# Spreading the second image's bottleneck samples over 210 samples of the next layer, with the image and offsets that follow moved after them

## The chip, the cores and the metric

The kernel runs on one core of one Trainium2 chip. The metric is the device time of one execution in microseconds (us). The core has five engines that this text names by their short names: PE (TensorE, matmuls), DVE (VectorE), ACT (ScalarE), POOL (GpSimd) and SP (SyncE, which only issues transfers here). Each runs its own instructions strictly in order and waits for the others by semaphores.

## The reference: what is computed

Four layers run one after another on two images (`B = 2`) of 256 channels and 64 x 64 pixels, in float32:

- L0: group norm, self-attention with 4 heads over the 4096 pixels, projection, residual.
- L1: a position term is added.
- L2: a bottleneck. A 1x1 convolution to 64 channels, then a 3x3 deformable convolution with a mask, a 1x1 convolution back to 256 channels, residual, ReLU.
- L3: two deformable convolutions of 256 channels, each behind a group norm and ReLU, and a residual at the end.

The part that this case is about is the deformable convolution. For each output pixel and each of 9 taps it samples the input at a learned place between pixels:

```python
out = gather(y0, x0) * (wy0 * wx0)[:, None] + gather(y0, x0 + 1.0) * (wy0 * wx1)[:, None] + gather(y0 + 1.0, x0) * (wy1 * wx0)[:, None] + gather(y0 + 1.0, x0 + 1.0) * (wy1 * wx1)[:, None]
```

The samples of all taps are then multiplied with the weights. The places come from an offset convolution over the normalised input.

## The kernel before, in words

The program has two stages. `attention` does L0 and L1 and, in its gaps, the bottleneck (L2) of image 0 and the first part of the bottleneck of image 1. `deform` does L3, and within it the rest of the bottleneck of image 1. The change is in `deform` alone.

**The samples.** `deform` is one loop over `s`. One value of `s`, called a sample here, is 128 pixels at one tap. A block of 512 pixels has 4 x 9 = 36 samples (`BLOCK = 36`), an image has 8 blocks, so one deformable convolution of one image has 288 samples (`LAYER = 288`). There are four of these: image 0 and image 1 of the first convolution, then both again for the second, 1152 samples in all. In iteration `s` the loop issues `gather(s + 8)` (four neighbours of 128 pixels, 512 KB, into one of 10 buffers `four`), `left(s + 3)` on ACT (line 1471), `right(s + 2)` on DVE (1477), `first(s + 1)` on ACT (1486), `others(s)` on DVE (1490 or 1496), two transposes of a sample on PE (1508), every fourth time a copy on ACT (1517), and the product with the weights on PE (1527). `left` and `right` exist for "paired" samples only; an unpaired one costs DVE three instructions of line 1496.

The first 72 samples (`EARLY * BLOCK`) were already gathered during the attention. They are loaded by plain transfers from `samp_d` (line 1448), and are unpaired. All later samples of the loop are gathered by POOL: one indirect transfer each (line 848).

**The side work.** Other work is written as generators and wrapped in `Side`. In each iteration `follow(s)` takes steps from the generator until their count reaches `rate * (s - start) + more(s)`. Nothing else schedules it: the order on each engine is the order in which the loop issues it.

- `second` is `Bottleneck.conv(1, ...)`, the deformable sampling of the bottleneck of image 1. It has 144 tiles of four neighbours. A tile is two indirect transfers on POOL into `bfour` (line 848), issued 7 tiles ahead, then three DVE instructions (1067, 1077, 1078), here called a weighing. It takes 7 steps for the first 7 tiles, then two steps per tile: one that issues the gather of the tile 7 further on and the first DVE instruction, one that issues the other two. Every 18 tiles, a block, products on PE and six more DVE instructions (1123, 1129, 1130) follow.
- `last` computes the places of the last two blocks of the same bottleneck, one step per sample.
- `offsets(b, l)` computes the places and shares of the next samples, 24 steps per block (`OFFS = 24`): 14 matmul steps (line 805), then seven small matmuls (825), four more (839) and small DVE arithmetic, ending in the indices `didx` (768). For image 0 of the first convolution it runs beside the samples at 24/36 of a step per sample. The next one in line, for image 1, begins at sample 228 at the same rate, so it ends at sample 516.
- `image(b, l)` loads and normalises an image (ACT, 1372), transposes it (PE, 1382), copies it (DVE, 1388) and writes it out to DRAM as `img3` (1394), from where the gathers read. For image 1 it begins when `second` is done, because it reuses its buffers (`inner.close()`) and needs its statistics.

Before the change `second` follows `0.9 s + 2.5 min(s, 72)`: 3.4 steps per sample over the first 72, then 0.9. It has about 300 steps, so its last tile is weighed at sample 127 and it ends at about sample 137. The image of image 1 follows at 0.9 of a step per sample, up to about sample 198.

Of the kernel before, what the change touches and what calls it, by code (L numbers as in the profile page):

```python
# [29 lines left out]
EARLY = 2  # L30
# [34 lines left out]
class Net:  # L65
# [1235 lines left out]
    def deform(self, bott):  # L1301
# [5 lines left out]
        with ExitStack() as ctx:  # L1307
# [19 lines left out]
            def load(b, src, pool):  # L1327
                x[b] = pool.tile([P, 2, HW], F32, name=f"x{b}")
                src = src.rearrange("(cb p) n -> p cb n", p=P)
                for i in range(4):  # L1330
                    cols = slice(1024 * i, 1024 * i + 1024)
                    queue = (nc.gpsimd, nc.sync)[b]
                    queue.dma_start(x[b][:, :, cols], src[:, :, cols])
# [3 lines left out]
            def offset_weights(l):  # L1337

                queue = (nc.gpsimd, nc.sync)[l]
                dw = wp.tile([P, 2, T], F32, name="dw")  # L1340
                queue.dma_start(dw, a["dw"][l])
                pw = wp.tile([P, 2, 2 * K2], F32, name="pw")
                queue.dma_start(pw, a["pw"][l])
                yield
                yield
                self.wf = wp.tile([P, 2, T, 2 * K2], F32, name="wf")
                for cb in range(2):
                    self.filters(self.wf[:, cb], cb, dw, pw)
                    yield
# [10 lines left out]
            def image(b, l):  # L1360

                if l == 0:
                    load(b, self.x2d[b], ctx.enter_context(tc.tile_pool(name="df_x1", bufs=1)))
                sc, sh = yield from self.norm_steps(
                    stats[b], bott.gmask, V_GN_G[l], V_GN_B[l], ps
                )
                yield
                v = self.img3[b].rearrange("(y x) (s c) -> y x s c", x=GW, c=C)
                for i in range(NB):
                    for cb in range(2):  # L1370
                        xs = x[b][:, cb, 512 * i : 512 * i + 512]
                        nc.scalar.activation(
                            xs, xs, AF.Relu, scale=sc[:, cb : cb + 1], bias=sh[:, cb : cb + 1]
                        )
                        yield
                    t = work.tile([P, 4, C], F32, name="imgt")
                    for g in range(2):
                        pt = ps([P, 2, C])
                        for j in range(2):
                            px = (4 * i + g * 2 + j) * P  # L1380
                            for cb in range(2):
                                nc.tensor.transpose(
                                    pt[:, j, cb * P : cb * P + P],
                                    x[b][:, cb, px : px + P],
                                    self.ident,
                                )
                        yield
                        nc.vector.tensor_copy(t[:, g * 2 : g * 2 + 2, :], pt)
                        if g == 1:
                            for r in range(2):  # L1390
                                for s in range(2):
                                    y0 = 8 * i + r + 1 - s
                                    dst = v[y0 : y0 + 7 : 2, 1 : W + 1, s, :]
                                    nc.sync.dma_start(
                                        dst.rearrange("j x c -> x j c"),
                                        t[64 * r : 64 * r + 64, :, :],
                                    )
                        yield

            IMAGE = 4 + 6 * NB + 1  # L1400
            corners = {(0, 0, i): (None, w4, None) for i, w4 in self.early.items()}

            def offsets(b, l):
                if b == 0:
                    yield from offset_weights(l)
                wf = self.wf
                for i in range(EARLY if (b, l) == (0, 0) else 0, NB):
                    idx = cp.tile([P, 4, K2], I32, name="didx")
                    w4 = cp.tile([P, 4, K2, 4], F32, name="dw4")
                    w = cp.tile([P, 2, 4, K2, 2], F32, name="dwt")  # L1410
                    corners[b, l, i] = idx, w4, w
                    yield from self.offsets(
                        i,
                        [x[b][:, cb, :] for cb in range(2)],
                        lambda s, row: wf[:, s, DWK * row : DWK * row + DWK, :].rearrange(
                            "p t o -> p (t o)"
                        ),
                        self.vec[:, V_PWB + l : V_PWB + l + 1],
                        base, idx, w4, work, ods[i % 2], pd, w=w,
                    )  # L1420
# [5 lines left out]
            layers = [(b, l) for l in range(2) for b in range(B)]  # L1426
            BLOCK = 4 * K2
            LAYER, ALL = NB * BLOCK, len(layers) * NB * BLOCK
            AHEAD, LEAD = 8, BLOCK + 16
# [8 lines left out]
            def gather(s):  # L1438
                if s < ALL:
                    n, i, k, j = parts(s)  # L1440
                    b, l = layers[n]
                    fours[s] = gp.tile([P, 4, C], F32, name="four")
                    four = fours[s].rearrange("p s c -> p (s c)")
                    if n == 0 and i < EARLY:

                        queue = nc.gpsimd if s < AHEAD else nc.sync
                        m = 4 * k + j
                        queue.dma_start(four, self.samp_d[i][m * P : m * P + P, :])
                        return
                    idx = corners[b, l, i][0]  # L1450
                    self.gather(four, self.img3[b], idx[:, j, k : k + 1])
# [15 lines left out]
            def left(s):  # L1467

                if paired(s):
                    uv = fours[s][:, 0:2].rearrange("p s c -> p (s c)")  # L1470
                    nc.scalar.mul(uv, uv, share(s, 0, 1))  # L1471

            def right(s):
                if paired(s):
                    four = fours[s].rearrange("p s c -> p (s c)")
                    uv = four[:, : 2 * C]
                    nc.vector.scalar_tensor_tensor(  # L1477
                        uv, four[:, 2 * C :], share(s, 1, 1), uv, ALU.mult, ALU.add
                    )
# [103 lines left out]
            OFFS = 24  # L1583
            inner = ExitStack()
            second = bott.conv(1, bott.pools(inner, 8, 7), ps)
# [7 lines left out]
            offs = [Side(EARLY * BLOCK - LEAD - 6, OFFS / BLOCK, begun)]  # L1593
# [1 line left out]


            last = Side(0, 1, bott.last(1, bott.kept, ps))
            seconds = Side(0, 0.9, second, lambda s: 2.5 * min(s, EARLY * BLOCK))
            stats[0] = self.norm_stats()
            images = []  # L1600
            for s in range(ALL + 12):
                n = s // LAYER
                if s == LAYER:
                    stats[1] = self.norm_stats()
                gather(s + AHEAD)
                left(s + 3)
                right(s + 2)
                first(s + 1)
                others(s)
                if (s - 6) % 4 == 0:  # L1610
                    evacuate((s - 6) // 4)
                product(*divmod(s - 7, 4), s)
                turn(s - 2)
                for f in due.pop(s, ()):
                    f()
                last.follow(s)
                if seconds:
                    seconds.follow(s)
                    if not seconds.steps:
                        seconds = None  # L1620
                        stats[1] = bott.stats[1]
                        inner.close()
                        images.append(Side(s, 0.9, image(*layers[1])))
                if s % LAYER == LAYER // 2 and 1 <= n < len(layers) - 1:
                    images.append(
                        Side(s, IMAGE / (LAYER // 2 - LEAD - 12), image(*layers[n + 1]))
                    )
                if s % LAYER == LAYER - LEAD - 8 and n + 1 < len(layers):
                    for o in images + offs:
                        for _ in o.steps or ():  # L1630
                            pass
                    images, offs = [], []
                    offs.append(Side(s, OFFS / BLOCK, offsets(*layers[n + 1])))
                for o in images + offs:
                    o.follow(s)

# [100 lines left out]
```

## Time and profile before

| what | value |
|---|---|
| median of three runs | 5140.26 us (5137.35 to 5144.84) |
| the profiled execution | 5136.46 us, span of the profile 5134.7 us |
| PE busy | 4802.3 us (94%) |
| DVE busy | 4012.2 us (78%) |
| ACT busy | 3255.6 us (63%) |
| POOL busy | 2336.0 us (45%) |

How to read it: line numbers are lines of the kernel before. Issuing a transfer counts as busy on POOL only where POOL itself builds it (lines 848, 1448, 1333, 1358). Line 1486 has one instruction per sample, 1152 in all, so the start of the n-th one, in order of time, says when sample n is reached. That gives this table, which the text uses to turn samples into times:

| sample | starts at, us from the start of the span |
|---|---|
| 0 | 2989.5 |
| 12 | 3036.8 |
| 72 | 3319.1 |
| 132 | 3492.6 |
| 204 | 3625.8 |
| 288 | 3759.7 |
| 432 | 3986.6 |
| 516 | 4126.0 |

### The profile page before, as it was taken

Reading aid. Unit: us, or ns where it says so; the run is one execution under the profiler, and the core shown is the slowest. Engines: PE = TensorE matmul, PEld = TensorE weight load, DVE = VectorE, ACT = ScalarE, POOL = GpSimd, SP = SyncE. Lnnn points to the kernel's source line nnn. Section 1 sums busy time; section 2 is a strip of 40 time slices with the busy share of each in tenths; the row PEclk is TensorE's granted clock in tenths of the full one; section 3 lists DMA queues with packets and bytes.
Section 4 is the critical chain, followed back from the end, with each engine's and each line's share of the span. In section 5 each row is a group of like instructions: output and inputs, shape, how many; then the busy total and the mean of one; then the engine's idle time right before and its main releaser. Section 6 shows DMA issues by size and latency. Waiting matters only on the chain. (4 is left out here: it accounts for less than half of the span.)

```text
span 5134.7 us, 100400 instructions
## 1 busy us (share of the span) xinstructions
PE 4802.3 (94%) x38200; PEld 2665.6 (52%) x38200; DVE 4012.2 (78%) x7281; ACT 3255.6 (63%) x5869; POOL 2336.0 (45%) x2256
## 2 busy tenths in 40 slices
PE   8999999999999999999999956679999999999998
PEld 5555565555565555565555523234444444454444
DVE  6878767878768888677766768867788888888888
ACT  5676656666667666666656622257876766666666
POOL 0111111111106777564023257775776666666665
PEclk9999999999999999999999978889999999999999
DMA  5231121111112333322557667679999999999998
GB/s 172 61 97 52 43 69 49 35 47 30 55 53 85 100 100 103 96 84 74 158 172 277 251 237 238 204 243 359 349 327 341 358 368 349 359 401 345 350 353 329
DMA packets 367026, 997.69 MB, mean 194 GB/s; under 512 B 61372, under 2 KB 98810, under 8 KB 366542
## 3 DMA queue, kind: packets, MB, share of 16 engines
q0 software_dynamic: 196560, 690.41, 37.7%
q1 hardware_dynamic: 169438, 300.73, 18.0%
q8 instruction: 300, 4.92, 0.4%
q14 instruction: 184, 1.51, 0.1%
q10 hardware_dynamic: 544, 0.13, 0.0%
HBM read 855.36 MB, written 127.35 MB: 191 GB/s over the span
## 5 line engine op out<-in xcount | busy, mean ns | idle before, releaser
L598 ACT ACTIVATE e<-sc,low 128x1024 f32<-128x1024 f32 x1024 | 1147.3, 1120 | 739.1 <-DVE low L592 736.2
L848 POOL DMA_INDIRECT four<-img,didx x1080 | 1163.2, 1077 | 558.1 <-issue 132.8
L592 DVE TENSOR_REDUCE low<-sc 128x1 f32<-128x1024 f32 x1024 | 1204.5, 1217 | 229.9 <-PE sc L580 225.3
L1527 PE MATMUL out<-st,wc 128*128 128x512 f32 x2304 | 1234.0, 618 | 118.2 <-ACT st L1517 100.7
L580 PE MATMUL sc<-k,qs 64*128 64x512 f32 x2048 | 998.0, 605 | 1.8 <-ACT e L598 1.4
L639 PE MATMUL av<-et,v 128*64 128x256 f32 x8192 | 996.6, 385 | 0.0
L580 PE MATMUL sc<-k,q 64*128 64x512 f32 x2048 | 977.0, 604 | 0.0
L519 POOL TENSOR_TENSOR o<-o,f 128x1024 f32<-128x1024 f32 x63 | 149.6, 2375 | 1763.4 <-DMA f<-share_d 966.5
L610 PEld LDWEIGHTS tt<-ident,e 64*128 64x128 f32 x16384 | 654.5, 139 | 512.4 <-issue 271.6
L629 ACT COPY et<-tt 128x512 f32<-128x512 f32 x1152 | 659.5, 585 | 171.4 <-PE tt L610 170.3
L1496 DVE SCALAR_TENSOR_TENSOR smp<-four,dw,smp 128x256 f32<-128x256 f32 x1296 | 627.2, 484 | 176.0 <-ACT smp L1486 144.9
L610 PE MATMUL tt<-ident,e 64*128 64x64 f32 x16384 | 726.5, 226 | 35.5 <-ACT et L629 18.3
L627 DVE COPY et<-tt 128x512 f32<-128x512 f32 x896 | 611.6, 683 | 161.7 <-PE tt L610 161.3
L639 PEld LDWEIGHTS av<-et,v 128*64 128x64 f32 x8192 | 553.2, 137 | 300.7 <-issue 47.8
L1508 PEld LDWEIGHTS pt<-ident,smp 128*128 128x128 f32 x2304 | 330.1, 144 | 661.6 <-issue 458.5
L848 POOL DMA_INDIRECT bfour<-img,bidx x576 | 583.5, 1013 | 183.5 <-issue 90.6
L1527 PEld LDWEIGHTS out<-st,wc 128*128 128x128 f32 x2304 | 389.9, 195 | 388.6 <-issue 201.2
L1471 ACT ACTIVATE four<-four,dwt 128x512 f32<-128x512 f32 x648 | 463.5, 715 | 192.6 <-DMA four<-img,didx 188.8
L1477 DVE SCALAR_TENSOR_TENSOR four<-four,dwt 128x512 f32<-128x512 f32 x648 | 483.8, 747 | 105.5 <-ACT four L1471 103.2
L1508 PE MATMUL pt<-ident,smp 128*128 128x128 f32 x2304 | 448.9, 277 | 27.2 <-DVE smp L1496 26.0
L580 PEld LDWEIGHTS sc<-k,qs 64*128 64x128 f32 x2048 | 346.2, 188 | 209.1 <-issue 116.3
L805 PE MATMUL pd<-x,wf 128*126 128x512 f32 x840 | 435.1, 600 | 0.0
(189 smaller groups left out, 4738.1 us busy)
## 6 DMA issues: line engine op xcount, KB each, us to landing
f<-share_d SPq DMA_DIRECT2D x128, 256.0 KB
four<-samp_d SPq DMA_DIRECT2D x64, 512.0 KB
xb<-xn SPq DMA_DIRECT2D x55, 512.0 KB
img<-imgt SPq DMA_DIRECT2D x96, 256.0 KB
four<-img,didx POOLq DMA_INDIRECT x1080
xa<-res SPq DMA_DIRECT2D x32, 512.0 KB
samp_d<-xb SPq DMA_DIRECT2D x32, 512.0 KB
xb<-in_x SPq DMA_DIRECT2D x20, 512.0 KB
```

The lines of the kernel that those rows point to most:

```text
L580: nc.tensor.matmul(s[:, j, :], lhsT=q[u, i // 2][int(h != j)][halves[j], at : at + P], rhs=k[u][c][halves[j], h, :], start=True, stop=True,)
L592: nc.vector.tensor_reduce(low, s, AX.X, ALU.max, negate=True)
L598: nc.scalar.activation(e.rearrange("p j n -> p (j n)"), s, AF.Exp, bias=blk.low[:, g, c : c + 1], accum_out=blk.sum[:, g, c : c + 1],)
L610: nc.tensor.transpose(pt[:, m, :], e[half, m // 4, m % 4 * P : m % 4 * P + P], self.ident[half, half],)
L627: nc.vector.tensor_copy(dst, pt)
L629: nc.scalar.copy(dst, pt)
L639: nc.tensor.matmul(now["av"][halves[h], :], lhsT=v[u][c][:, m, halves[h]], rhs=ets[j][:, m, h, :], start=(m == 0), stop=(m == 7),)
L848: self.nc.gpsimd.indirect_dma_start(out=dst, out_offset=None, in_=img, in_offset=bass.IndirectOffsetOnAxis(ap=idx, axis=0),)
L1477: nc.vector.scalar_tensor_tensor(uv, four[:, 2 * C :], share(s, 1, 1), uv, ALU.mult, ALU.add)
L1496: nc.vector.scalar_tensor_tensor(smps[s], four[:, c], weight(s, c), smps[s], ALU.mult, ALU.add)
L1508: nc.tensor.transpose(pts[u][:, c, j * P : (j + 1) * P], smp[:, c * P : c * P + P], self.ident,)
L1527: nc.tensor.matmul(outs[ob], lhsT=wc[k][:, c, ob * P : ob * P + P], rhs=sts[u][:, c, :], start=(k == 0 and c == 0), stop=(k == K2 - 1 and ...
```

## The change

Three paces are changed, all of side work in `deform`; no instruction's size or engine is.

- `second` follows a pace of its own: 8 steps at once at sample 0, none until sample 10, 1.95 per sample up to sample 72 (129 steps by then), then 1.25 per sample. By it the last tile's gather is issued at about sample 197, its last weighing at sample 206, and `second` ends at about sample 212.
- The image of image 1 follows at `IMAGE / (OPEN - END)` = 53/48 = 1.10 steps per sample, from about sample 212 to 261.
- The offsets of image 1 begin at sample 262 (`OPEN`) and no longer at 228: the 24 steps of the first block in 16 samples, the rest at 0.85 per sample, so they end at about sample 476. The later layers' offsets keep their start and rate.

```diff
-            seconds = Side(0, 0.9, second, lambda s: 2.5 * min(s, EARLY * BLOCK))
+            HELD, END, OPEN = 10, 214, LAYER - 26
+
+            def pace(s):
+
+                early, late = min(s, EARLY * BLOCK), max(0, s - EARLY * BLOCK)
+                return 8 + 1.95 * max(0, early - HELD) + 1.25 * late
+
+            def offset_pace(s):
+
+                return OFFS * min(1, (s - OPEN) / 16) + 0.85 * max(0, s - OPEN - 16)
+
+            seconds = Side(0, 0, second, pace)
...
-                        images.append(Side(s, 0.9, image(*layers[1])))
+                        images.append(Side(s, IMAGE / (OPEN - END), image(*layers[1])))
...
-                if s % LAYER == LAYER - LEAD - 8 and n + 1 < len(layers):
+                if s == OPEN or s % LAYER == LAYER - LEAD - 8 and 0 < n < len(layers) - 1:
...
-                    offs.append(Side(s, OFFS / BLOCK, offsets(*layers[n + 1])))
+                    if s == OPEN:
+                        offs.append(Side(s, 0, offsets(*layers[1]), offset_pace))
+                    else:
+                        offs.append(Side(s, OFFS / BLOCK, offsets(*layers[n + 1])))
```

## The prediction

> **What bounds the kernel now.** I read the page first, then turned samples into times (the start of the n-th instruction of line 1486), cut the answer by windows at those times, and read the groups of the window where the change takes most away.
>
> ```profile
> span 5134.7 us, 100400 instructions
> ...
> PE   8999999999999999999999956679999999999998
> ...
> DVE  6878767878768888677766768867788888888888
> ...
> POOL 0111111111106777564023257775776666666665
> PEclk9999999999999999999999978889999999999999
> ```
>
> One slice is 128 us. Only in slices 23 to 27, the beginning of the sample loop, does PE fall; there POOL and DVE are highest. Windows, columns PE, PEld, DVE, ACT, POOL busy (instructions), PE clock, DMA share, GB/s:
>
> ```profile
> 2989.50:3036.80 47.30, 16.09 (x42) 8.31 (x41) 28.09 (x70) 9.70 (x20) 27.77 (x30) 0.54 0.83 300
> 3036.80:3319.10 282.30, 189.56 (x589) 86.13 (x588) 250.98 (x579) 68.87 (x128) 218.43 (x210) 0.80 0.70 221
> 3319.10:3437.10 118.00, 77.33 (x240) 36.73 (x239) 77.94 (x167) 53.80 (x93) 91.47 (x87) 0.84 0.71 227
> 3492.60:3609.00 116.40, 107.70 (x414) 55.07 (x413) 86.56 (x178) 95.52 (x166) 63.98 (x61) 0.97 0.98 370
> 3625.80:3759.70 133.90, 129.15 (x459) 63.57 (x458) 98.97 (x201) 111.92 (x197) 100.25 (x85) 1.00 0.91 335
> 3759.70:3986.60 226.90, 219.54 (x777) 105.87 (x776) 190.99 (x428) 153.57 (x270) 152.27 (x145) 1.00 0.93 334
> 5057.80:5107.30 49.50, 41.47 (x144) 20.15 (x144) 45.77 (x92) 35.67 (x64) 37.91 (x37) 1.00 1.02 400
> ```
>
> Samples 12 to 72 take 282.3 us: 210 transfers on POOL, 1.344 us each, though one is busy for only 1.04: some 0.3 us of issue follows each. In samples 72 to 108 it is 118.0 / 87 = 1.356. POOL's 0.77 busy is thus saturation, and 1.35 us is its price of a gather. DVE is 0.89 busy in the same 282 us. From sample 204 on (3625.8) PE is 0.965 busy and sets the pace.
>
> Groups of samples 12 to 72 (busy, mean ns | idle before):
>
> ```profile
> L848 POOL DMA_INDIRECT bfour<-img,bidx x207 | 215.8, 1043 | 63.1 <-issue 32.3 <-DVE smp L1496 8.5 <-DMA bfour<-img,bidx 7.6
> L1496 DVE SCALAR_TENSOR_TENSOR smp<-four,bw,smp 128x256 f32<-128x256 f32 x184 | 88.9, 483 | 4.4
> L1067 DVE TENSOR_TENSOR bfour<-bfour,bw 128x512 f32<-128x512 f32 x105 | 71.9, 685 | 14.5 <-DMA bfour<-img,bidx 14.4
> L1077 DVE TENSOR_TENSOR bfour<-bfour 128x256 f32<-128x256 f32 x105 | 44.4, 423 | 2.6
> L1078 DVE TENSOR_TENSOR bsmp<-bfour 128x128 f32<-128x128 f32 x105 | 30.7, 293 | 8.7
> ```
>
> A weighing costs DVE 0.685 + 0.423 + 0.293 = 1.40 us, an unpaired sample 3 x 0.483 = 1.45. DVE's largest idle here, 14.4 us, is for gathers that POOL brings late.
>
> **The change part by part.**
>
> *A, samples 0 to 72, now 329.6 us.* At the start the 8 steps at sample 0 hold the first weighing, so on DVE it stands ahead of sample 1, and waits there for its gather, which today lands at:
>
> ```profile
> 3014.28 0.69 DVE L1067 TENSOR_TENSOR bfour<-bfour,bw 128x512 f32<-128x512 f32 x1 [16.50 <-DMA bfour<-img,bidx]
> ```
>
> Behind it wait samples 1 to 10, and through them PE. Fewer sample loads run ahead of that gather, so I take 3011; ten samples and some 4 us of corner arithmetic follow, and sample 12 starts at 3029, not 3036.8 (3024 to 3036).
> Samples 12 to 72 on DVE: 60 x 1.45 = 87; 59 weighings x 1.40 = 83; 3.3 block ends x 2 x (0.745 + 0.481 + 0.694, the rows of lines 1123, 1129 and 1130) = 13; corner arithmetic about 10; together 193. The same sum for the kernel before gives 87 + 147 + 22 + 13 = 269 against 251.0 measured, as neighbours overlap; so 193 x 0.93 = 180. Without the 14.4 us of late gathers DVE's idle would be 17 in 282, so 0.94 busy: 191 us (180 with no idle, 203 at today's 0.89). POOL needs (118 + 8) x 1.35 = 170 meanwhile, and hides. Sample 72 starts at 3220: **-99 us**.
>
> *B, samples 72 to 204, now 306.7 us.* The image leaves this stretch (samples 132 to 193 took 116.4 us with it, line four of the windows) and weighings fill it. By sample 72 the steps have issued 68 tiles, 136 transfers; 152 remain, and 132 own gathers: 284 x 1.35 = 383 us on POOL. DVE has per 12 samples 12 x (0.747 + 0.480), the rows of lines 1477 and 1490, + 7.5 x 1.40 and some 4 more, 29 against 2.25 x 12 x 1.35 = 36, so POOL sets the pace. A gather is issued eight samples ahead and first read five later, so POOL may fall behind before it hurts; I take off 8 (0 to 15): 375. The price lies between 0.94 + 0.30 = 1.24, with DVE idle (352 in all), and 1.085 + 0.336 = 1.42, the mean of the own gathers from 3319 to 3490 (403). I keep 1.35, from the window nearest in mix. Sample 204 at 3595: **+68**.
>
> *C, samples 204 to 288, now 133.9 us.* Today this stretch holds no image; now it takes it in. PE without offsets is busy 41.47 / 36 = 1.152 per sample (last window above, samples 1104 to 1140), with 0.667 step 219.54 / 144 = 1.525, so an offset step is 0.56. Sum: 84 x 1.152 = 96.8; 22 steps left of the first offsets 12.3; 32.5 steps of the next 18.2; the image's 64 transposes 10.4 (row of line 1382); tail of `second` 3; together 140.7, at 0.965 busy 146. The same sum for today (no image, 40 steps of the next offsets, 131.5 at 0.965) gives 136; 133.9 were measured. To it comes the image's own stall, at its load, today hidden nowhere:
>
> ```profile
> 3517.31 0.81 ACT L1372 ACTIVATE x<-x,gn_sh,gn_sc 128x512 f32<-128x512 f32 x1 [6.77 <-issue]
> ```
>
> Behind it wait ACT's shares, then DVE, then POOL's next gather: 9 us. Samples 237 to 262 are not PE-bound: 0.70 MB per sample (gather and image) at some 400 GB/s is 1.75 against 1.42: 8. C is 163 (148 to 180): **+29**. SP issues the four writes per image block as before; the last leave at sample 261, and the gathers that read them start at 280, over 25 us later: nothing.
>
> *D, samples 288 to 516.* To 432, PE has 1.152 + 0.85 x 0.56 = 1.628 a sample, at 0.968 busy 1.68; 144 of them 242 against 226.9, +15. From 432 the offsets end early (476) beside the next image; the time that PE then stands unsaturated about equals the steps saved: -1. **+14** (0 to 20).
>
> The sum is -99 + 68 + 29 + 14 = **+12 us**. The profiled execution took 5136.5, so 5148.5; the median of the runs shown stands 3.8 above it: **5152 us**. Under 0.2% (10.3 us) a measurement of this kernel can hardly tell from none.
>
> **Rules weighed.** PE's granted clock is 0.80 to 0.84 in the two POOL-bound windows, and B lengthens such a stretch. [...]
>
> **The rivals.**
> - *PE has slack late.* If the late pace is set by gathers, ACT and DVE (ACT is 0.84 busy from 3625.8), PE's added steps in C and D cost nothing: C falls by 12, from 146 to today's 134 before its stall and its slow stretch, D by 14, and the sum is -14: 5126. Against it stands PE at 0.965. It turns the sign once more than 12 of the 26 us vanish.
> - *Gathers get cheaper.* At 1.24 B falls by 284 x 0.11 = 31, and the sum is -19: 5121. For it: single transfers of 0.94 us when DVE idles; against it the two equal prices. It turns the sign below 1.31 us.
> - *DVE is held up in A.* Its in-order waits (for ACT's first product, PE's banks) keep it at 0.86 and not 0.94 busy: 209 us, +18: 5170. For it: 0.89 today; against: 14.4 us of today's idle is POOL's.
>
> **How the numbers follow.** The forecast has 0.60, its own range 5132 to 5170 (A, B and C each uncertain by some 10): slower 0.40, within 0.2% 0.16, faster 0.04. PE slack 0.17: faster 0.13, same 0.04. Cheap gathers 0.10: faster 0.08, same 0.02. DVE held up 0.13, slower. Together faster 0.25, same 0.22, slower 0.53. The range goes from just under the two faster rivals, 5116, to 5182, the third rival with B at 1.39.
>
> **What would show it.** Sample 72 near 3220 with DVE over 0.92 busy and POOL's gathers hidden (A); samples 72 to 194 at POOL 0.77 busy and 1.35 us a gather, near 2.9 us each (B); sample 288 some 163 us after 204 with the stall at line 1372 (C); 1.68 us per sample from 288 to 432 (D). I am wrong if DVE isn't the limit in A, if B's gathers cost other than 1.35, or if C stays near 140.

## The result, and the profile after

The changed kernel takes 5177.39 us (median, 5172.06 to 5179.72) where the kernel before takes 5141.51 us (5137.35 to 5149.18) on the same chip: a ratio of 1.007, 95% interval 1.0058 to 1.0081. It is slower by 0.7%. Its profiled execution took 5179.27 us, 42.8 above that of the kernel before; 30.8 above the 5148.5 that the sum of the prediction gives for it. The median stands 25 above the predicted 5152, inside the range given for all cases and 7 above the forecast's own range (5132 to 5170). The direction came as forecast, and the change is three times the forecast one: +12 us were predicted, +36 came between the medians.

The page of the changed kernel, in the same rows as before the change (one slice is 129 us):

```profile
span 5177.5 us, 100285 instructions
...
PE   8999999999999999999999967677899989999998
...
DVE  6878767878678888687766679667778888888888
...
POOL 0111111111107777473022267777566666666666
PEclk9999999999999999999999979888999999999999
```

The dip of PE, four slices at 5, 6, 6 and 7 before the change, has become shallower and longer: six at 6, 7, 6, 7, 7 and 8, with a single eight further on. The windows by sample show it in time. They are samples 0 to 12, 12 to 72, 72 to 204, 204 to 216, 216 to 262, 262 to 288 and 288 to 432 of the changed kernel; the columns are PE, PEld, DVE, ACT and POOL busy (instructions), PE clock, DMA share, GB/s:

```profile
2991.10:3026.00 34.90, 12.03 (x34) 5.75 (x32) 15.53 (x40) 8.66 (x17) 17.93 (x20) 0.54 0.95 351
3026.00:3210.20 184.20, 139.48 (x464) 60.13 (x464) 174.84 (x420) 59.06 (x107) 122.54 (x115) 0.93 0.78 258
3210.20:3620.60 410.40, 290.15 (x901) 137.72 (x901) 288.44 (x623) 202.35 (x344) 319.60 (x299) 0.83 0.74 235
3620.60:3654.50 33.90, 26.64 (x101) 12.97 (x99) 20.62 (x48) 21.04 (x37) 14.04 (x14) 0.96 0.85 318
3654.50:3738.40 83.90, 71.53 (x278) 38.54 (x277) 64.02 (x126) 71.22 (x124) 47.29 (x44) 0.92 1.02 382
3738.40:3787.20 48.80, 46.88 (x166) 23.07 (x165) 31.39 (x68) 34.07 (x60) 31.25 (x26) 1.00 0.81 287
3787.20:4028.30 241.10, 235.19 (x831) 113.62 (x830) 194.07 (x443) 155.49 (x272) 152.75 (x148) 1.00 0.91 318
```

The windows of the kernel before for samples 72 to 204, 204 to 216, 216 to 262 and 262 to 288, which the prediction did not show apart:

```profile
3319.10:3625.80 306.70, 244.81 (x866) 121.09 (x865) 221.40 (x475) 200.20 (x346) 208.46 (x195) 0.91 0.86 303
3625.80:3643.60 17.80, 17.80 (x61) 8.93 (x60) 13.07 (x24) 15.51 (x29) 12.98 (x13) 1.00 1.01 398
3643.60:3716.90 73.30, 71.06 (x269) 35.21 (x268) 55.62 (x117) 62.67 (x112) 52.70 (x46) 1.00 0.90 323
3716.90:3759.70 42.80, 40.28 (x132) 19.44 (x131) 30.29 (x61) 33.74 (x59) 34.57 (x28) 1.00 0.89 330
```

By the starts of line 1486 the stretches of the prediction come out so (us; 42.8 in all):

| samples | before | predicted change | after | change |
|---|---|---|---|---|
| A, 0 to 72 | 329.6 | -99 | 219.1 | -110.5 |
| B, 72 to 204 | 306.7 | +68 | 410.4 | +103.7 |
| C, 204 to 288 | 133.9 | +29 | 166.6 | +32.7 |
| D, 288 to 516 | 366.4 | +14 | 382.0 | +15.6 |
| the rest | | 0 | | +1.3 |

So the order of things is as forecast, and the sum is off by B. One count says more than the table. In the windows of samples 0 to 204 POOL has 30 + 210 + 195 = 435 instructions in the kernel before and 20 + 115 + 299 = 434 in the changed one (gathers, but for three or four loads of image 0 at the start), and these 204 samples take 636.3 and 629.5 us. The change spreads the same transfers and gains 6.8 us in the stretch that holds them. The image, which it moved out of that stretch, and the offsets, which it moved back behind the image, cost 48 us in the two stretches that follow.

### The profile page after: what moved, and what is told of

The parts are those of the page before. It is cut to its first block, busy times and chain, and to the rows that moved or that the text cites. A ratio compares the mean times of both kernels' runs of the same rounds, so it can differ in the third digit from the quotient of the medians.

```text
span 5177.5 us, 100285 instructions
## 1 busy us (share of the span) xinstructions
PE 4817.4 (93%) x38200; PEld 2670.2 (52%) x38200; DVE 4009.9 (77%) x7281; ACT 3260.2 (63%) x5869; POOL 2333.5 (45%) x2256
## 5 line engine op out<-in xcount | busy, mean ns | idle before, releaser
L1527 PE MATMUL out<-st,wc 128*128 128x512 f32 x2304 | 1249.9, 626 | 198.5 <-ACT st L1517 182.5
L1471 ACT ACTIVATE four<-four,dwt 128x512 f32<-128x512 f32 x648 | 463.7, 716 | 309.4 <-DMA four<-img,didx 307.0
```

The costliest lines, as they stand in the source:

```text
L1527: nc.tensor.matmul(outs[ob], lhsT=wc[k][:, c, ob * P : ob * P + P], rhs=sts[u][:, c, :], start=(k == 0 and c == 0), stop=(k == K2 - 1 and ...
```

## The experiments

Every ratio is against the kernel before on the same chip, since chips differ: the experiments ran on three others, and on two of them the kernel before itself takes 5300 and 5319 us instead of 5141, which the last section comes to. The second column names the chip by its time of the kernel before, and stretches are compared between kernels of one chip. The stretches of all runs (us):

| kernel | chip's before | 0-12 | 12-72 | 72-204 | 204-288 | 288-432 |
|---|---|---|---|---|---|---|
| before | 5141.5 | 47.3 | 282.3 | 306.7 | 133.9 | 226.9 |
| after | 5141.5 | 34.9 | 184.2 | 410.4 | 166.6 | 241.0 |
| after_again | 5300.2 | 36.3 | 209.7 | 435.5 | 164.0 | 241.1 |
| hold_7 | 5300.2 | 20.2 | 193.0 | 443.4 | 163.0 | 241.3 |
| two_corners | 5300.2 | 34.3 | 198.5 | 432.3 | 171.1 | 241.0 |
| loads_on_sp | 5300.2 | 44.2 | 346.8 | 316.0 | 139.3 | 229.2 |
| offsets_only | 5319.3 | 47.4 | 346.5 | 304.2 | 141.1 | 242.8 |
| offsets_even | 5319.3 | 36.0 | 213.8 | 440.5 | 164.6 | 240.3 |
| early_2p6 | 5319.3 | 35.4 | 264.1 | 410.7 | 146.5 | 241.2 |
| half_plain | 5319.3 | 36.2 | 213.7 | 349.2 | 166.3 | 242.4 |
| after_ahead | 5143.8 | 36.3 | 186.1 | 405.0 | 168.3 | 241.0 |
| hold7_ahead | 5143.8 | 21.1 | 188.3 | 408.9 | 161.6 | 241.0 |
| before_ahead | 5143.8 | 47.4 | 282.9 | 305.2 | 130.0 | 227.2 |
| before_hold | 5143.8 | 20.2 | 304.7 | 307.0 | 133.9 | 226.9 |

### What bounds the spread stretch: half of its transfers taken from POOL

```diff
+                        if b == 1 and n >= 68 and m == 1:
+                            nc.sync.dma_start(fours[n][:, m].rearrange("p s c -> p (s c)"), net.img2[b][0 : 2 * P].rearrange("(p u) f -> p (u f)", u=2))
+                            continue
                         net.gather(fours[n][:, m].rearrange("p s c -> p (s c)"), net.img2[b], self.idx[b, i][:, j, k : k + 1])
```

The second gather of the late tiles becomes a plain load of the same size on SP's queue, so those tiles hold other data than the indices ask for.

> The changed kernel; from the 69th tile of the bottleneck on (those issued behind sample 72) the second of a tile's two gathers is a plain transfer of the same bytes from fixed rows, issued by SP, so that POOL has one transfer per tile less; those samples are therefore not the reference's. Nothing else differs: DVE, PE and the bytes moved are the same. If POOL's issue bounds samples 72 to 204: some 76 transfers fewer, 410 us fall to DVE's bound, about 315. If the bound is DVE, PE or the landing of the gathers, it stays within 20 us of 410.

One execution, 5253.37 us. Samples 72 to 204 took 349.2 us against 440.5 in offsets_even, which is the same kernel up to sample 278 on the same chip: 91 us less for 76 transfers fewer on POOL, 1.2 us each, while the same bytes moved (211 GB/s in 440.5 us and 269 GB/s in 349.2 us are both some 93 MB). Some 315 us, DVE's bound, were expected. The windows of samples 72 to 204, first offsets_even, then half_plain:

```profile
3300.40:3740.90 440.50, 288.89 (x905) 137.46 (x904) 279.58 (x613) 200.49 (x346) 307.45 (x288) 0.79 0.67 211
3300.50:3649.70 349.20, 265.14 (x904) 126.50 (x903) 277.12 (x613) 200.07 (x346) 231.85 (x212) 0.87 0.80 269
```

POOL is down to 0.66 busy, and DVE with 0.79 is now the busiest engine, PE next with 0.76. So it is the issue on POOL, and not the bytes, that sets the pace of B; this much of the prediction holds. The plain loads read the same fixed rows each time, so an easier landing is not ruled out as a part of the 1.2 us.

### The changed kernel again, and the wait at its start: 8 steps or 7

The changed kernel was run again (after_again), on the chip of hold_7, two_corners and loads_on_sp. In hold_7 the first weighing is no longer among the steps at sample 0:

```diff
-                return 8 + 1.95 * max(0, early - HELD) + 1.25 * late
+                return 7 + 1.95 * max(0, early - HELD) + 1.25 * late
```

> The changed kernel as it is, beside the others of this call. The forecast's theory: 0.6 to 0.8% slower than the kernel before, as where it was first measured; stretches of 184 us (samples 12 to 72), 377 (72 to 192) and 167 (204 to 288) in an execution without stalls in instruction issue. If the cost comes from something that such stalls hide, the ratio is nearer to 1.

> The changed kernel with 7 steps at sample 0 instead of 8: the first weighing moves from before sample 1 on DVE to behind sample 10, everything of the bottleneck one step later. If DVE's wait there holds up samples 1 to 10, samples 0 to 12 fall from 35 us to about 25, and the later stretches keep their lengths: 8 to 12 us less than the changed kernel. If the wait is hidden (weights or sample loads are as late), under 3 us.

after_again: 5302.44 us, ratio 1.0009 (0.9994 to 1.0024), so on that chip the change costs nothing that can be measured, where 0.6 to 0.8% were expected; see the last section. hold_7: 5280.68 us, 0.9965 (0.9952 to 0.9978), 22 us under after_again. Windows of samples 0 to 12 of after_again, then of samples 0 to 12 and 12 to 72 of hold_7:

```profile
3044.50:3080.80 36.30, 12.17 (x33) 6.00 (x32) 15.75 (x41) 8.74 (x17) 18.10 (x20) 0.53 0.91 335
3044.70:3064.90 20.20, 13.56 (x39) 6.53 (x38) 18.09 (x49) 8.85 (x18) 8.22 (x10) 0.66 1.04 407
3064.90:3257.90 193.00, 141.51 (x458) 61.30 (x458) 173.44 (x411) 58.17 (x106) 132.47 (x125) 0.89 0.81 268
```

Without that weighing DVE does 18.09 us of work in the first 20.2; with it, 15.75 in 36.3. The wait of the eighth step at the head of DVE's queue thus costs 16 us, and the prediction's A had it right that it stands there. The whole gain is twice the 8 to 12 us expected. Samples 12 to 72 are 17 us shorter too and 72 to 204 8 us longer; the same edit on another chip (hold7_ahead against after_ahead, below) has them 2 and 4 us longer, so only the first 12 samples repeat.

### Is DVE the limit in A: one addition less per sample

```diff
-                    for c in range(1, 4):
+                    for c in range(1, 4 if s >= EARLY * BLOCK else 3):
```

This leaves the fourth corner out of the first 72 samples.

> The changed kernel; in the first 72 samples DVE leaves out the last of the three additions of line 1496 (those samples lack one of their four neighbours, so they are not the reference's). If DVE bounds samples 12 to 72, they fall by 60 x 0.483 x 0.93 = 27 us, down to POOL's 115 transfers x 1.37 = 158 at the lowest, from 184; samples 72 to 192, bound by POOL, keep their 377 us or take up to 10 more because POOL is further behind. If something else bounds samples 12 to 72, they stay within 8 us of 184.

One execution, 5297.17 us; samples 12 to 72 took 198.5 us against 209.7, 11 less, where 27 were expected with DVE as the limit and under 8 with another: a miss of both. Windows of samples 12 to 72, first after_again, then two_corners:

```profile
3080.80:3290.50 209.70, 142.45 (x458) 61.36 (x459) 176.87 (x425) 58.74 (x108) 130.94 (x124) 0.88 0.75 242
```

```profile
3082.80:3281.30 198.50, 138.20 (x459) 62.43 (x458) 146.16 (x356) 58.32 (x108) 127.12 (x125) 0.86 0.77 255
```

DVE lost 30.7 us of work, and 11 us of time came of it. The groups of two_corners in that window (busy, mean ns | idle before) say what took over:

```profile
L1496 DVE SCALAR_TENSOR_TENSOR smp<-four,bw,smp 128x256 f32<-128x256 f32 x121 | 58.6, 484 | 29.2 <-ACT smp L1486 20.5 <-issue 6.5
...
L1486 ACT ACTIVATE smp<-four,bw 128x256 f32<-128x256 f32 x60 | 28.6, 505 | 24.3 <-PE pt L1508 14.1 <-issue 4.4 <-remote 3.8
```

DVE now waits for ACT's first product and ACT for the transposes of PE (20.5 and 14.1 us, against 6.2 and 9.7 in after_again). On this chip DVE was 0.84 busy in these samples before the edit, so it is the limit for a part of the time only, and the next one stands close behind. On the first chip, where DVE is 0.95 busy, the edit was not run; that it is the limit there rests on the trace.

### The offsets alone, and their pace

offsets_only is the kernel before with nothing changed but the offsets of image 1 (from sample 262 at 0.85 per sample, in the changed kernel's lines):

```diff
-                if s % LAYER == LAYER - LEAD - 8 and n + 1 < len(layers):
+                if s == OPEN or s % LAYER == LAYER - LEAD - 8 and 0 < n < len(layers) - 1:
...
-                    offs.append(Side(s, OFFS / BLOCK, offsets(*layers[n + 1])))
+                    if s == OPEN:
+                        offs.append(Side(s, 0, offsets(*layers[1]), offset_pace))
+                    else:
+                        offs.append(Side(s, OFFS / BLOCK, offsets(*layers[n + 1])))
```

offsets_even is the changed kernel with a slower pace after the first block of offsets:

```diff
-                return OFFS * min(1, (s - OPEN) / 16) + 0.85 * max(0, s - OPEN - 16)
+                return OFFS * min(1, (s - OPEN) / 16) + 0.706 * max(0, s - OPEN - 16)
```

> The kernel before, with only the offsets of image 1 moved (start at sample 262, first block in 16 samples, then 0.85 a step); the bottleneck's samples and the image keep their paces of before. If PE sets the late pace (the forecast's C and D): samples 288 to 432 take 241 us and not 226.9, 204 to 288 about 3 us more than 133.9, 432 to 516 the same; together +14 to +18 us on the kernel before. If PE has slack there (rival), the change is under 3 us.

> The changed kernel, with 0.706 of an offset step per sample after the first block instead of 0.85, so that they end at sample 516 again. If PE sets the pace: 288 to 432 takes 144 x (1.152 + 0.706 x 0.56) / 0.968 = 230 us and not 241, 432 to 516 0 to 3 us more: 8 to 11 us less than the changed kernel. If PE has slack: no difference.

offsets_only: 5325.97 us, 1.0013 (1.0002 to 1.0023), some 7 us (1 to 12) above the kernel before, where 14 to 18 were expected with PE as the limit and under 3 without. offsets_even: 5327.89 us, 1.0012 (1.0001 to 1.0024). Windows of samples 288 to 432, offsets_only first:

```profile
3884.50:4127.40 242.90, 235.76 (x832) 113.66 (x831) 194.45 (x443) 155.21 (x272) 153.79 (x148) 1.00 0.90 317
```

```profile
3905.40:4145.70 240.30, 226.45 (x787) 108.59 (x786) 192.45 (x428) 153.58 (x269) 153.65 (x146) 0.99 0.90 320
```

Moving the offsets alone brings 242.9 us for samples 288 to 432, as in the changed kernel: that part of D stands by itself. The whole grew by about half of what was expected; no kernel with the old offsets was traced on this chip, so where the rest went is open. But the slower pace took 9.3 us of PE's work out of the same stretch and only 2.6 us of time, where some 10 were expected. That PE sets the pace here, step by step, is therefore shown in one direction only: added steps cost, steps taken away did not come back. In offsets_even PE waits 11.5 us for ACT's copies (line 1517), in offsets_only 6.1; why is open.

### Weighing faster early: 2.6 steps and not 1.95

```diff
-                return 8 + 1.95 * max(0, early - HELD) + 1.25 * late
+                return 8 + 2.6 * max(0, early - HELD) + 1.25 * late
```

> The changed kernel, with 2.6 steps per sample instead of 1.95 up to sample 72, so 40 steps (40 transfers, 20 weighings) go from behind sample 72 to before it. If DVE bounds samples 12 to 72 and POOL bounds 72 to 192 at 1.37 us a transfer: 12 to 72 rises from 184 to about 217, 72 to 204 falls from 410 to about 357, 204 to 288 falls by about 15 because the image starts some 35 samples sooner; together about 35 us less than the changed kernel, near the kernel before. If samples 72 to 192 are bound by something other than POOL's transfers (DVE, PE, latency between them), the two stretches about cancel: within 10 us of the changed kernel but for the image.

5332.76 us, 1.002 (1.0005 to 1.0036): 5 us above offsets_even, where some 35 us less than the changed kernel were expected, a miss. Windows of samples 12 to 72 of offsets_even, then of samples 12 to 72, 72 to 204 and 204 to 288 of early_2p6:

```profile
3086.70:3300.40 213.70, 151.13 (x458) 63.94 (x457) 176.40 (x423) 58.65 (x107) 130.61 (x124) 0.82 0.73 236
3081.00:3345.10 264.10, 167.06 (x510) 75.79 (x510) 205.53 (x484) 61.66 (x115) 170.56 (x161) 0.78 0.66 211
3345.10:3755.80 410.70, 275.91 (x917) 132.98 (x918) 267.45 (x590) 203.38 (x352) 263.24 (x251) 0.82 0.71 234
3755.80:3902.30 146.50, 132.47 (x477) 66.72 (x476) 104.47 (x212) 116.93 (x205) 93.31 (x83) 0.97 0.91 335
```

Against offsets_even on the same chip A grew by 50 us and B and C fell by 30 and 18. By sample 72 POOL had issued 37 transfers more, and paid for them in A at 50 / 37 = 1.36 us each. B, with 37 transfers fewer, gave back 30 us, 0.8 each. So a transfer moved from B to A is paid in full in A, and comes back from B in part only; the image begins at sample 182 there and takes some of B, which the run does not separate.

### The start of the loop in the kernel before: two loads on SP, and the held start alone

loads_on_sp issues the loads of two lines (the weights and image 0, 13 transfers) from SP instead of POOL in the kernel before; before_hold gives the kernel before the held start of the changed one, with 7 steps, and the same 245 steps by sample 72:

```diff
-                    queue = (nc.gpsimd, nc.sync)[b]
+                    queue = nc.sync
...
-                queue = (nc.gpsimd, nc.sync)[l]
+                queue = nc.sync
```

```diff
-            seconds = Side(0, 0.9, second, lambda s: 2.5 * min(s, EARLY * BLOCK))
+            seconds = Side(0, 0.9, second, lambda s: 7 - 0.9 * min(s, 10) + 2.94 * max(0, min(s, EARLY * BLOCK) - 10))
```

> The kernel before, with the loads of the weights (line 1358) and of image 0 (line 1333) at the start of the loop issued by SP instead of POOL. If POOL's stream of gathers bounds everything up to about sample 108, as the forecast reads it, the 13 loads taken off POOL and the landings that POOL waits for behind them let its first gather start some 8 to 20 us sooner, and the whole is 8 to 20 us shorter than the kernel before. If DVE is as much the bound there, or the data are late anyway, under 5 us.

> The kernel before, whose second is held like in the changed kernel: 7 steps at sample 0, none up to sample 10, then 3.84 a sample up to 72, the same 245 steps by then. Samples 0 to 72 issue the same transfers as before. If POOL's gathers bind them, the wait removed at the start comes back: 0 to 12 falls from 47 to some 22, 12 to 72 rises by 16 transfers x 1.35 = 22, the sum unchanged within 6 us. If DVE's wait at the first weighing is what costs, the sum falls by 15 to 25.

loads_on_sp: 5295.24 us, 0.999 (0.9975 to 1.0004), no gain that can be told, where 8 to 20 us were expected if POOL's earlier start were all that counts; the rival's "under 5" fits. before_hold: 5145.49 us, 1.0004 (0.9995 to 1.0013). Its windows of samples 0 to 12 and 12 to 72:

```profile
2993.30:3013.50 20.20, 13.41 (x39) 6.49 (x38) 18.09 (x49) 8.84 (x17) 9.48 (x10) 0.65 1.04 407
3013.50:3318.20 304.70, 198.57 (x591) 89.17 (x590) 260.09 (x596) 70.09 (x129) 232.72 (x227) 0.76 0.69 222
```

This run is the plainest of all. The wait at the start is gone (47.3 to 20.2 us, -27), and 12 to 72 is longer by 22.4, which is 227 - 210 = 17 transfers at 1.32 us. Where POOL's transfers are the limit, 27 us saved on DVE are worth next to nothing.

### Is C bound by PE: the first offsets earlier

The offsets of image 0 run at 1.0 step per sample from sample 58 and not at 0.667, in the changed kernel (after_ahead), in hold_7 (hold7_ahead) and in the kernel before (before_ahead):

```diff
-            offs = [Side(EARLY * BLOCK - LEAD - 6, OFFS / BLOCK, begun)]
+            offs = [Side(EARLY * BLOCK - LEAD - 6, 1.0, begun)]
```

> The changed kernel with the offsets of image 0 (first convolution) at 1.0 step per sample from sample 58 instead of 0.667, so that they end at sample 202 and not at 274; everything else as in the changed kernel. If the spread stretch (samples 72 to 204) is bound by POOL's gathers and samples 204 to 288 by PE, the steps moved ahead are hidden in the first and saved in the second: 72 to 204 unchanged within 4 us, 204 to 288 from some 165 to some 153 (22 steps x 0.56 = 12 less), 288 on unchanged; the whole 10 to 14 us under the changed kernel, a ratio of about 0.998 of the kernel before on a chip where the changed kernel is at 1.0009. Rival, PE is not the limit from 204 to 288 (the image's load and stall are): 204 to 288 unchanged. Rival, PE at its lower clock is a limit from 72 to 204 too: that stretch 10 to 20 longer.

> The same earlier offsets together with 7 instead of 8 steps of second at sample 0. The two edits act in different stretches (0 to 72, and 204 to 288), so their gains should add: samples 0 to 12 at some 20 and not 36, 204 to 288 at some 153; 10 to 14 under the kernel with 7 steps alone (0.9965), a ratio of 0.993 to 0.995 of the kernel before. If only one of the two holds, 0.996 to 0.998.

> The kernel before with the offsets of image 0 at 1.0 step per sample. Here samples 132 to 204 are not bound by POOL alone (PE 0.93 busy, the image in it), so only the steps moved into samples 58 to 132 are hidden: 204 to 288 falls by 8 to 12, 132 to 204 grows by 6 to 12; the whole -6 to +2 us, 0.999 to 1.0004. If POOL still sets the pace up to 204 the whole falls by 12 us, 0.9977.

after_ahead: 5179.59 us, 1.0065 (1.0052 to 1.0079), no better than the changed kernel on the first chip (1.007). Its windows of samples 204 to 216, 216 to 262 and 262 to 288:

```profile
3623.00:3661.50 38.50, 25.95 (x86) 12.37 (x85) 21.24 (x51) 20.93 (x37) 15.71 (x15) 0.78 0.89 316
3661.50:3742.50 81.00, 67.88 (x249) 36.05 (x249) 61.43 (x110) 70.30 (x122) 48.20 (x43) 0.90 1.01 379
3742.50:3791.40 48.90, 46.97 (x166) 23.12 (x165) 31.46 (x69) 34.23 (x61) 31.19 (x26) 1.00 0.81 293
```

The steps are gone from C (PE has 501 instructions there, and not 545) and C takes 168.4 us, not 12 less than 166.6. PE's busy time fell by 4.3 us only, from 145.1 to 140.8, beside a lower clock in samples 204 to 216 (0.78, where the changed kernel has 0.96). In 216 to 262 PE is 0.84 busy and the DMA engines 1.01. The rival named in the expectation holds: up to sample 262 PE is not the limit.

hold7_ahead: 5161.17 us, 1.0031 (1.0019 to 1.0043), 18 under after_ahead; the expected ratio of 0.993 to 0.995 was carried over from a chip on which the changed kernel costs nothing, and missed, and hold_7 itself was not run on this chip. Its samples 0 to 12 took 21.1 us, 15 less; C took 161.6. The held start is worth as much on this chip as on the other, and the change with it is still slower than the kernel before.

before_ahead: 5139.15 us, 0.9988 (0.9979 to 0.9997), faster than both kernels, if by less than the 0.2% that the prediction took as telling. Its windows of samples 72 to 204 and 204 to 288:

```profile
3326.00:3631.20 305.20, 241.96 (x873) 119.44 (x872) 222.13 (x475) 200.96 (x345) 209.98 (x195) 0.92 0.86 305
3631.20:3761.30 130.10, 122.72 (x415) 59.87 (x414) 95.99 (x186) 109.97 (x196) 99.64 (x85) 0.97 0.94 346
```

The steps cost nothing where they went (305.2 us, against 307.0 in before_hold on the same chip), and gave 3.8 us where they had been (130.1 against 133.9), less than half of the 8 to 12 expected.

## Why the prediction was right, and where it was off

**The sign and the order of the terms** were right: A gains some 100 us, and B, C and D give more than that back. It is the forecast's mechanism that came in A and B, and not a rival's; B is where its size was missed, and C came to its size by another way. That 5177 lies inside the whole range is luck in part: the upper end, 5182, was set for DVE held up in A, which did not come, and what came in its place were B's 35 us.

**A.** Sample 12 came at 3026.0, three before the 3029 predicted, and sample 72 at 3210.2, not 3220. The groups of samples 12 to 72 of the changed kernel:

```profile
L848 POOL DMA_INDIRECT bfour<-img,bidx x111 | 118.4, 1066 | 65.2 <-DVE bsmp L1078 40.0 <-issue 21.9 <-DVE smp L1496 0.9
L1496 DVE SCALAR_TENSOR_TENSOR smp<-four,bw,smp 128x256 f32<-128x256 f32 x185 | 89.3, 483 | 4.6 <-issue 0.2
...
L1067 DVE TENSOR_TENSOR bfour<-bfour,bw 128x512 f32<-128x512 f32 x58 | 39.7, 684 | 0.0
```

DVE is 174.84 / 184.2 = 0.95 busy, against the 0.94 that the sum used, and its wait for late gathers is gone (0.0 us before line 1067, and 14.5 before the change). The first line is what the prediction overlooked. POOL stood idle 40.0 us for line 1078: it gathers seven tiles ahead into eight buffers, and the next one is free only when DVE has weighed an older tile. "POOL needs (118 + 8) x 1.35 = 170 meanwhile, and hides" was true of A and asked the wrong thing. POOL was the limit of the next stretch, so what it did not issue in A, B had to make up. How much of it these waits account for is not shown, since no run has more buffers; the nearest is hold7_ahead, where the wait for line 1078 in these samples is 18.4 us and not the 38.8 of after_ahead, and samples 0 to 204 take 9 us less, with the start changed too.

**B is the step that failed**: "By sample 72 the steps have issued 68 tiles, 136 transfers; 152 remain, and 132 own gathers: 284 x 1.35 = 383 us on POOL", less 8, "375". The trace has 127 of those 136 transfers issued on POOL by sample 72, and 4 own gathers, not the 8 that the loop is ahead by: 13 of its transfers were still to come. The window of B has 299 and not 284 (the other two lie at its edges), and they took 410.4 us, 1.373 us each. The 35 us between are 15 transfers x 1.35 = 20, a price higher by 0.023 x 299 = 7, and the 8 us that were taken off for POOL falling behind. POOL entered B late already, so there was nothing of this kind left to take off. Part of the first came back, since A was 11 shorter than predicted; for A and B together the sum said 605.5 us and 629.5 were measured. That POOL's issue is the limit was right (half_plain), and 1.35 us was a fair price. The groups of samples 72 to 192 show where the rest of the price sits:

```profile
L848 POOL DMA_INDIRECT bfour<-img,bidx x154 | 166.1, 1078 | 46.9 <-issue 29.6 <-DVE bsmp L1078 5.5 <-DVE smp L1490 3.7
...
L848 POOL DMA_INDIRECT four<-img,didx x120 | 128.5, 1071 | 36.6 <-issue 16.1 <-ACT four L1471 6.4 <-ACT smp L1486 6.1
...
L1471 ACT ACTIVATE four<-four,dwt 128x512 f32<-128x512 f32 x120 | 86.6, 722 | 184.3 <-DMA four<-img,didx 183.9
```

Besides 1.07 us busy and about 0.17 of issue, POOL waits a little for the buffers of both kinds (5.5, 3.7, 6.4 and 6.1 us are the named ones). The last line is the other end: ACT waits 183.9 us in this stretch for gathers.

**C** was 166.6 us and predicted at 163, but not for the reasons given. "together 140.7, at 0.965 busy 146" has PE setting the pace. By the windows PE does so only from 262 to 288 (0.96 busy, 6.0 us more than before, with the block of 24 offset steps). Samples 204 to 216 took 16.1 us more than before, with the end of `second` and the image's start in them, where the stall was forecast at 9 and the tail at 3. Two rows of ACT there show the stall, 5.45 us long (start, us long, idle before); the rest of the 16.1 is not taken apart:

```profile
3644.57 0.49 ACT L1486 ACTIVATE smp<-four,dwt 128x256 f32<-128x256 f32 x1
3650.51 0.81 ACT L1372 ACTIVATE x<-x,gn_sh,gn_sc 128x512 f32<-128x512 f32 x1 [5.45 <-issue]
```

Samples 216 to 262 took 10.6 us more beside DMA engines whose share is 1.02 (0.90 before the change); that fits the term of "8" for 237 to 262, if a little too small, and no run tests it. after_ahead shows the PE terms to be wrong here: with the first offsets gone from C, "22 steps left of the first offsets 12.3" saved nothing. That C came out within 4 us of its forecast is luck: the two errors balanced.

**D** was +14.1 us for 288 to 432, where +15 was predicted, and +1.5 for 432 to 516, where -1 was; offsets_only comes near the same 241.0 us by itself, with 242.8 on another chip. The price of one step is less certain than that agreement makes it look, by offsets_even.

**The rivals.** "PE has slack late" is half right: true up to sample 262, false behind it, and no saving came of it, as the stall and the transfers of 204 to 262 took the time. "Gathers get cheaper" fell: 1.373 us, not 1.24. Nor is 1.24 a price "with DVE idle": in the kernel before, seven gathers in a row from 3015 to 3023 us take 0.94 or 0.95 us each, 0.30 apart, while DVE is busy nearly throughout. "DVE is held up in A" fell: DVE was 0.95 busy.

**The clock, and the price of a gather.** The clock in B was 0.83, as in the two POOL-bound windows of the kernel before (0.80 and 0.84); since half_plain finds POOL's issue at the limit, no part of B's 35 us need be the clock's. A gather cost 1.344 us beside a DVE that is 0.89 busy (samples 12 to 72 of the kernel before), 1.356 beside one at 0.66 (samples 72 to 108 of it) and 1.373 beside one at 0.70 (B): the price did not follow DVE's share.

## What to carry to other kernels

When work is spread over a longer stretch, count the instructions of the limiting engine up to the point where the stretch ends, in the old order and in the new: here 435 and 434, so nothing but idle time of POOL could be won, and the image and the offsets, moved behind that stretch, were the price of the 7 us gained. An engine that is hidden in one stretch and the limit of the next one must not be allowed to wait in the first, and how far it can run ahead is set by its buffers as well as by its pace: this is read from POOL's waits in A (40.0 us for line 1078), and no run with more buffers was made. Steps that an engine is spared are worth their price only where that engine is shown to wait for nothing else: PE's steps priced at 12 us, taken from C, and 27 us of DVE's wait, taken from the kernel before, each came to about nothing. A like wait at the start of the changed kernel, where POOL is not the limit of samples 12 to 72, was worth 18 and 22 us.

## What the hardware showed that was not expected

The same program differs between chips by 3%. The kernel before takes 5141 and 5144 us on two chips and 5300 and 5319 us on two others. About 53 us of the difference lie ahead of sample 0, and most of the rest where POOL gathers without a break: samples 12 to 72 of its code take 346.5 us (offsets_only, loads_on_sp) and not 282.3, with single instructions as long as in the kernel before on the first chip (in offsets_only 484 ns for line 1496 on DVE, 765 for line 1527 on PE and 1033 for a gather of line 848; there 483, 778 and 1043). In that time engines stand still for long after what they wait for is there. Rows of PE, then of ACT, of the changed kernel on the slower chip (after_again):

```profile
3266.49 4.10 PE L1098 MATMUL pm<-bst,w 128*64 128x256 f32 x20 [5.13 <-issue]
```

```profile
3266.34 0.51 ACT L1486 ACTIVATE smp<-four,bw 128x256 f32<-128x256 f32 x1
3285.64 1.14 ACT L1110 ACTIVATE bst<-pm,bn_t,bn_s 64x256 f32<-64x256 f32 x2 [18.80 <-remote]
```

Line 1110 needs the product of line 1098, which ended at 3270.6; it starts 15 us later, and no event in the trace releases it. Adding up all idle times over 0.5 us on ACT that no event of the trace ends gives 23 us for the same kernel on the first chip and 279 us here. Nothing in the records explains it, and its cause stays open. The parity of the two kernels there, 1.0009, goes with it: from sample 12 to 288 the code of the kernel before (loads_on_sp, the same but for two loads at its start) loses 64, 9 and 5 us in the three stretches of the table, the changed one 25, 25 and -3. A change of this kind has to be measured beside the kernel before on one chip, and its ratio is not carried from one chip to another.
